# Statistics of the next image half a key block earlier, and sums of weight forms tied to running sums, in a fused GroupNorm and attention kernel

## The chip, the cores and the metric

The kernel runs on one core of one Trainium2 chip. The metric is the device time of one execution in microseconds (us); of several runs the median is taken. The engines are called PE (TensorE, the matmuls), PEld (its weight loads), DVE (VectorE), ACT (ScalarE), POOL (GpSimd) and SP (SyncE, which here only issues DMAs). Each of them runs its own instructions strictly in the order in which the compiled program has them, and waits on semaphores for the others.

## What is computed

One attention block over 16 images of 512 channels and 32 x 32 = 1024 positions, all in 32-bit floats:

```
x: (16, 512, 32, 32)
xn = GroupNorm(x, 8 groups) * gamma + beta
qkv = einsum('oc,bchw->bohw', qkv_w, xn) + qkv_b        # 1536 x 512 weights
q, k, v = 4 heads of 128 channels, 1024 positions each
attn = softmax(q k^T / sqrt(128))
out = proj_w (attn v) + proj_b                          # 512 x 512 weights
return x + out
```

## The kernel before

**The main loop.** The work on the scores sets the rhythm. A *step* is one block of 128 keys of one head of one image; 16 images x 4 heads x 8 blocks make 512 steps. A step has two halves of 512 queries each. In every half PE computes the scores `s` of this step (line 1669) and the weighted sum `po` of the step before (line 1766); ACT takes the exponential `p` of the scores (line 1675); DVE adds each full `p` to the running sum `tot` of the head (lines 1688 and 1690), from which the softmax denominators come. Between the scores and weighted sums of a half, PE gets its share of the other matrix products: the q, k and v products of the next image and the output projection (`pp`) of the previous image. These use fast matrix multiplication (Strassen's scheme on two levels for images 0 to 3, a scheme with three by three by two blocks, `thirds`, from image 4 on), so they need many sums: of input blocks (`home_A`, `home_B`, on DVE), of weights, and of products (`pp_r`, `qk_r`, `v_r`, on DVE), and copies out of PSUM on ACT (`pp_u`, `pp_z` and others, lines 655, 821 to 828).

**Which head does what.** For an image b of 1 to 14, head 0 finishes the q and k products of image b. Head 1 runs the 28 units of the projection of image b - 1, loads `x` of image b + 1, and takes that image's GroupNorm. Heads 2 and 3 run products for image b + 1.

**GroupNorm of the next image.** `stats_chunk` handles one of four chunks of 128 channels on ACT: a pass with an accumulated sum (line 329), two tiny scalings, and a pass with accumulated squares (line 335). Both passes write to a scrap tile `junk`. `stats_group` then has two parts on DVE. `gather` (lines 357 to 363) brings the results of all chunks together, combines them and ends with a power on POOL; it is bound behind the running sum of key block 3 of head 1. `scale` (lines 367 to 101) makes the factors `sc` and `sh`, bound behind the running sum of block 4. The eight normalisations (line 108, ACT) multiply and shift halves of each chunk, and use `sc` and `sh`.

**Weight forms.** Images 0 to 3 also build the weights for `thirds`, in spare tiles. `form_steps` makes sums of weight blocks, called forms: it loads blocks, adds six forms (line 1505), stores them (line 1512), adds five more in the same places, and stores these. There are four such chunks, in heads 3, 4, 6 and 7 (heads counted from the start; head 4 is head 0 of image 1). `inner_steps` takes eleven groups of forms: a load of a group (through `load_quads`, lines 1521 and 1533, SP), the making of four inner sums (lines 1541 to 1544, DVE) and a store (line 1562, POOL). The groups belong to heads 5, 8, 9, 10, 11, 12 and 13. `lay_builder` writes these steps into slots of half a key block, with the load four or five halves ahead of the sums.

**What sets the order.** The program text gives every instruction a place, but the order on each engine is made when the program is compiled: a planner goes through a model of the execution and lets each engine take, of what would be ready by its reckoning, what comes first by priority and place. So an instruction may be put ahead of its place in the text when the planner reckons that its inputs are there and the engine is free. `tc.issue_after(ins)` binds the instructions of a block that run on the engine of `ins` behind it in that engine's order; the helper `behind(one, unit)` does so for a unit, and `behind_exp` binds it behind the newest exponential. `tc.high_priority` moves an instruction forward among those that are ready. `added[b, h, j]` is the running sum of image b, head h, key block j (from block 2 on), and `max(added)` is the newest one that the text has reached.

**The plan of a head.** `plan_head` returns eight lists, one for each key block. The first half of a list runs after the first half of the step, the rest after the second. Empty entries (`None`) hold the lists at equal lengths. In head 1 the list of block 2 has four empty entries and that of block 3 three; the four statistics units go into these lists.

Of the kernel before, what the change touches and what calls it, by code (L numbers as in the profile page):

```python
# [231 lines left out]
def fast_path(ctx, tc, x, sources, out, consts, flag, dims):  # L232
# [1231 lines left out]
    def quads(n):  # L1464

        t = builder["tiles"]
        return t[n // 4][:, n % 4]
# [13 lines left out]
    def form_steps(p, c):  # L1481
        made = {}

        def load():
            for m, base in enumerate((0, 2 * C, C)):
                nc.sync.dma_start(
                    builder["tiles"][m // 2][:, ds(2 * (m % 2), 2)],
                    qkv_wT[:, ds(base + p * Q + c * P, P)].rearrange(
                        "(r k p) d -> p r k d", p=P, k=KC
                    ),  # L1490
                )

        def slot(f):
            k = order_a.index(f) % 6
            return quads(8 + k if k < 4 else 2 + k)

        def add(first, last):

            def of(what):
                return quads(2 * what[0] + what[1]) if isinstance(what, tuple) else made[what]  # L1500

            for f, op, a, e in FORMS_A[first:last]:
                eng = nc.vector
                made[f] = slot(f)
                (eng.tensor_add if op == "+" else eng.tensor_sub)(made[f], of(a), of(e))

        def send(first, last):
            for i in (first, first + 4):
                e = min(last, i + 4 if i == first else last)
                t = builder["tiles"][2 if i % 6 == 0 else 1]  # L1510
                t = t[:, : e - i] if i % 6 == 0 else t[:, ds(2, e - i)]
                nc.sync.dma_start(forms_kept[p, c][:, i:e], t)

        return (
            load, lambda: add(0, 6), lambda: send(0, 6), lambda: add(6, 11), lambda: send(6, 11)
        )

    def load_quads(p, g, c, w, eng):
# [50 lines left out]
    def lay_builder():  # L1569

        def at(head, half, step):
            s, h = divmod(half + 16 * head, 2)
            extras.setdefault((s, h), []).append(step)

        if old == B:
            return
        at(HEADS, 4, lambda: behind(added[max(added)], sum_biases))
        chunks = [(p, c) for p in range(PAIRS) for c in range(2)]
        for head, where, firsts, last in BUILD_A:
            if where:  # L1580
                at(head, firsts[0], lambda where=where: take(where))
            for first in firsts:
                for i, step in zip((0, 4, 7, 11, 14), form_steps(*chunks.pop(0))):
                    at(head, first + i, step)
            if last:
                at(head, 15, builder.clear)
        assert not chunks
        groups = [divmod(G, len(THIRDS)) for G in range(LATE)]
        turn = 0
        for run_ in BUILD_B:  # L1590
            first = True
            for head, where, firsts in run_:
                if where:
                    at(head, firsts[0] - 1, lambda where=where: take(where))
            slots = [
                16 * head + f for head, where, firsts in run_ for f in firsts
            ]
            mine, groups = groups[: len(slots)], groups[len(slots):]
            steps = []
            for k, (p, g) in enumerate(mine):  # L1600
                steps.append(inner_steps(p, g, k % 2))
            for k, t in enumerate(slots):
                load, make, send = steps[k]
                at(0, t, load)
                at(0, t + 5, make)
                at(0, t + 5, send)
            at(0, slots[-1] + 5, builder.clear)
        assert not groups
# [42 lines left out]
    inverse, rows_of, added, exps = {}, {}, {}, {}  # L1651
# [323 lines left out]
    def behind(one, unit):  # L1975
        with tc.issue_after(one.ins):
            unit()
# [4 lines left out]
    def plan_head(b, h):  # L1982

        plan = [[] for _ in range(NB)]
# [21 lines left out]
        elif h == 1:  # L2006
            if b > 0:
                spread(plan, [None] * 28, 0, NB)
                halfway.extend(paced(proj_groups(b - 1), 3))
                if flow:  # L2010
                    halfway[0] = flow.pop() + halfway[0]
            if b + 1 == B:
                plan[0].append(lambda: last_loads("x"))
            else:
                chunks = range(NCC) if b > 0 else range(KC, NCC)
                plan[0].append(lambda: load_x(b + 1, chunks))
                units = [
                    lambda c=c: behind_exp(lambda: stats_chunk(b + 1, c)) for c in chunks
                ]
                if b > 0:  # L2020
                    for i, u in enumerate(units):
                        plan[2 + i // 2].insert(0 if i % 2 == 0 else len(plan[2]), u)
                else:
                    spread(plan, units, 1, 3)
                gather, scale = stats_group(b + 1)
                if b == 0:
                    plan[3].append(gather)
                    plan[4].insert(0, scale)
                else:
                    plan[4].insert(0, gather)  # L2030
                    plan[5].insert(0, scale)
                for r in range(2):
                    units = [
                        lambda c=c, half=half: normalise(b + 1, c, half, b > 0 or c % 2 == 1)
                        for c in range(KC * r, KC * r + KC) for half in range(NH2)
                    ]
                    plan[5 + r] += units if b > 0 else [
                        lambda u=u: behind_exp(u) for u in units
                    ]
                if b + 1 < old:  # L2040
                    plan[6].append(lambda: x_sums(b + 1, (1,)))
            if b == 0:
                for part in range(2):
                    plan[1 + part].append(lambda part=part: behind(
                        latest["worst"], lambda: keep_kept("v", part, nc.sync)
                    ))
                plan[5].append(stage_proj)
        elif b + 1 == B:
            if h == 2:
                units = two_levels("last", "proj", b, lambda: late["two"], None)[0]  # L2050
                late["units"] = units[2:]
                products(plan, units[:2], NB, "last 2")
                plan[0].append(lambda: last_loads("w"))
                plan[0].append(ahead["last", "w"])
                plan[2].append(last_bias)
                plan[5].append(lambda: first_pair(b))
            else:
                os_[b, h] = opool.tile([P, N], F32, tag="o", name=f"o_{b}_{h}")
                products(plan, late["units"], NB, "last 3")
                plan[3].append(lambda: first_terms(b, 0))  # L2060
                plan[3].append(lambda: o_blocks(b))
                plan[4].append(lambda: first_terms(b, 1))
                plan[5].append(lambda: sums_of_b(ob[b], (2, 3), (0,)))
        elif b + 1 >= old:
            if h == 2:
                flow.extend(thirds(b + 1))
                spread(plan, [None] * 37, 0, NB)
                halfway.extend(flow[:16])
                del flow[:16]
        elif h == 2:  # L2070
            if b == 0:
                other_banks()
            spread(plan, [None] * 28, 0, NB)
            halfway.extend(paced(qk_groups(b + 1, 0), 4))

            plan[0].insert(2, lambda: x_sums(b + 1, (2,)))
            plan[1].append(lambda: x_sums(b + 1, (3,)))
            if b == 0:
                plan[3].append(lambda: behind(added[0, 2, 2], sum_proj))
                plan[4].append(  # L2080
                    lambda: behind(added[0, 2, 3], lambda: keep_kept("proj", 0, nc.gpsimd))
                )
        else:

            spread(plan, [None] * 28, 0, NB - 1)
            halfway.extend(paced(next_v.pop(), 3))

            plan[NB - 2].append(lambda: ahead[f"qk_{b + 1}_1"]())
            if b == 0:
                plan[1].append(lambda: keep_kept("proj", 1, nc.gpsimd))  # L2090
# [213 lines left out]
    plan = []  # L2304
    for s in range(steps + 1):
        units = []
        if s < steps:
            b, h, j = where(s)
            if j == 0:
                left = carry.pop() if carry else []  # L2310
                plan = plan_head(b, h)
# [9 lines left out]
        for half in range(NH2):  # L2321
# [21 lines left out]
            n = (len(units) + 1) // 2  # L2343
# [158 lines left out]
```

## Time and profile before

| | us |
|---|---|
| median of 3 runs (lowest, highest) | 3149.41 (3147.36, 3150.98) |
| the profiled execution | 3149.29 |
| its span, first to last instruction | 3147.7 |
| PE busy | 3115.7 |
| DVE busy | 2695.5 |
| ACT busy | 1724.7 |
| POOL busy | 471.1 |

The span lies 1.6 us under the time of the same execution. All lines of profile in this text come from that one execution; times in them count from its first instruction. A line of a timeline has the start, the length, the engine, the line of the kernel, the operation, the tiles (out<-in) with their shapes, the number of equal instructions merged into the row, and in brackets the idle time of the engine before it with what ended it. A row of the waits has who waited for whom, the total, the number of times and the longest. Matmuls of PE overlap each other, and so a row's length is longer than its share of the time: what counts is the distance between starts.

### The profile page before, as it was taken

The numbers are of one execution on the slowest core, as the hardware profiler recorded it, in microseconds if no ns is written. First come the engines' busy times: TensorE is split into PE (matmuls) and PEld (weight loads), VectorE is DVE, ScalarE is ACT, GpSimd is POOL, SyncE is SP. The second block draws the span as 40 slices with busy tenths as digits, with TensorE's granted clock in tenths as the row PEclk, the third lists the DMA queues.
The fourth block names the chain that finished last, engine by engine and source line by source line (L and its number), as shares of the span: only waits on it lengthen the run. The fifth ranks groups of instructions, "written<-read, shape, count | busy, mean of one in ns | idle before, by whom it ended". The sixth has DMA issues, their size and how long they took to land.

```text
span 3147.7 us, 38210 instructions
## 1 busy us (share of the span) xinstructions
PE 3115.7 (99%) x11934; PEld 2262.3 (72%) x11934; DVE 2695.5 (86%) x4604; ACT 1724.7 (55%) x3744; POOL 471.1 (15%) x792
## 2 busy tenths in 40 slices
PE   9999999999999999999999999999999999999999
PEld 7566676767777777777777777777777777777775
DVE  8987978789898897888978889788897888989887
ACT  3544546446565565656556565565555656556543
POOL 0121121121021110211102111121111111111110
PEclk9999999999999999999999999999999999999999
DMA  5566764665767656676666666676666666666761
GB/s 177 177 219 195 242 219 163 214 208 190 226 219 210 212 193 207 212 224 196 200 197 223 218 198 199 194 233 208 201 201 206 222 209 197 211 208 205 222 193 45
DMA packets 244062, 636.78 MB, mean 202 GB/s; under 512 B 32656, under 2 KB 77840, under 8 KB 243856
## 3 DMA queue, kind: packets, MB, share of 16 engines
q1 hardware_dynamic: 164912, 363.58, 37.3%
q0 software_dynamic: 66272, 236.38, 22.2%
q10 hardware_dynamic: 12672, 34.35, 3.7%
q8 instruction: 96, 1.57, 0.2%
q14 instruction: 110, 0.90, 0.1%
HBM read 462.49 MB, written 171.69 MB: 201 GB/s over the span
## 4 chain that ended last, share of the span: by engine, by line
PE 61%; ACT 5%; DVE 3%; issue 2%; DMA 0%; POOL 0%; ACTq 0%; POOLq 0%
PE s L1669 18%; PE po L1766 18%; PE t_x L1237 12%; PE t_y L1237 6%; PE t_z L1237 3%; PE pp_x L780 2%; ACT junk L329 1%; PE pp_y L780 1%; ACT junk L335 1%; DVE tot L1690 1%; ACT p L1675 1%; ACT x L108 1%; DVE pp_r L887 0%; PE pp_z L780 0%; DVE o L1779 0%
## 5 line engine op out<-in xcount | busy, mean ns | idle before, releaser
L1766 PE MATMUL po<-p,v 128*128 128x512 f32 x2048 | 1046.2, 592 | 0.0
L1669 PE MATMUL s<-qk,qk 128*128 128x512 f32 x2048 | 1046.0, 592 | 0.0
L1766 PEld LDWEIGHTS po<-p,v 128*128 128x128 f32 x2048 | 616.1, 301 | 376.2 <-issue 259.7
L1675 ACT ACTIVATE p<-s 128x512 f32<-128x512 f32 x1024 | 611.6, 597 | 498.7 <-PE s L1669 494.5
L1690 DVE TENSOR_TENSOR tot<-tot,p 128x1024 f32<-128x1024 f32 (+1 forms) x408 | 471.2, 1156 | 178.7 <-ACT p L1675 176.4
L1669 PEld LDWEIGHTS s<-qk,qk 128*128 128x128 f32 x2048 | 362.2, 189 | 59.1 <-issue 29.4
L1261 DVE TENSOR_TENSOR r<-t_y,t_u 128x342 f32<-128x342 f32 (+1 forms) x384 | 185.0, 482 | 138.1 <-PE t_y L1237 111.0
L1352 DVE TENSOR_TENSOR r<-r,r 128x684 f32<-128x684 f32 x264 | 225.7, 862 | 1.7
L1237 PE MATMUL t_x<-home_B,w 128*128 128x171 f32 x1008 | 187.7, 308 | 0.0
L1237 PE MATMUL t_x<-home_A,w 128*128 128x171 f32 x1008 | 187.7, 308 | 0.0
L1237 PEld LDWEIGHTS t_x<-home_A,w 128*128 128x128 f32 x1008 | 161.7, 189 | 30.2 <-issue 20.1
L1237 PEld LDWEIGHTS t_x<-home_B,w 128*128 128x128 f32 x1008 | 161.7, 189 | 30.2 <-issue 20.1
L780 PE MATMUL pp_x<-home_B,w_proj 128*128 128x256 f32 x630 | 168.3, 384 | 14.6 <-ACT pp_u L828 13.8
L1330 POOL DMA_DIRECT2D vd<-vu x48 | 34.8, 728 | 955.2 <-DVE vu L1322 955.2
L1061 POOL DMA_DIRECT2D v<-vd x240 | 140.7, 592 | 191.9 <-DMA x<-in_x 57.4
L780 PEld LDWEIGHTS pp_x<-home_B,w_proj 128*128 128x128 f32 x630 | 117.4, 190 | 59.2 <-ACT pp_u L828 23.7
L1124 DVE TENSOR_TENSOR f<-x 128x684 f32<-128x684 f32 x168 | 143.9, 856 | 0.8
L1197 ACT COPY t_u<-t_x 128x342 f32<-128x342 f32 x192 | 78.7, 410 | 118.9 <-PE t_x L1237 112.6
L1237 PEld LDWEIGHTS t_z<-f,w 128*128 128x128 f32 x528 | 89.5, 190 | 51.8 <-issue 34.4
L108 ACT ACTIVATE x<-x,sh,sc 128x512 f32<-128x512 f32 x120 | 92.6, 809 | 27.7 <-DVE sh L101 26.0
L1322 DVE STREAM_TRANSPOSE vu<-vt 128x256 f32<-128x256 f32 x192 | 104.2, 643 | 0.0
L1203 ACT ACTIVATE t_u<-t_x,bias 128x171 f32<-128x171 f32 x192 | 72.3, 404 | 57.1 <-PE t_x L1237 57.0
(383 smaller groups left out, 5107.4 us busy)
## 6 DMA issues: line engine op xcount, KB each, us to landing
w<-kept SPq DMA_DIRECT2D x182, 512.0 KB, 3.9
w<-kept SPq DMA_DIRECT2D x182, 384.0 KB, 4.1
kept_t<-home_A POOLq DMA_DIRECT2D x96, 342.0 KB, 3.9
home_B<-kept_t SPq DMA_DIRECT2D x96, 342.0 KB, 3.0
rinv<-row ACTq DMA_DIRECT2D x63, 512.0 KB, 5.7
x<-in_x POOLq DMA_DIRECT2D x60, 512.0 KB, 8.3
v<-vd POOLq DMA_DIRECT2D x240, 128.0 KB, 7.3
out_y<-y_c POOLq DMA_DIRECT2D x60, 512.0 KB, 3.9
```

The source lines that it names most:

```text
L108: return self.nc.scalar.activation(xn, x, AF.Identity, bias=sh[:, i], scale=sc[:, i])
L780: latest["product"] = nc.tensor.matmul(acc[:, ts(i, Q)], have["w"][t][:, i, slot, :], inner(i, bn), start=(first and i == 0), stop=True, s ...
L1061: nc.gpsimd.dma_start(vs[b, pair][ts(q, BLK), half].rearrange("m h (k i) j -> m (h k) (i j)", k=n), rows.rearrange("(k m) (q e) -> q m k e ...
L1124: (eng.tensor_add if op == "+" else eng.tensor_sub)(made[f], of(a), of(c))
L1237: latest["product"] = nc.tensor.matmul(acc[:, ts(i, H3)], wts[G, t][:, i, slot, :], moving, start=(start and i == 0), stop=True, skip_grou ...
L1261: nc.vector.tensor_add(dst, view(a), view(c))
L1322: nc.vector.transpose(u[:, h].rearrange("p (q i j) -> p j q i", q=n, i=BLK)[:, ds(2 * q, 2)], made["vt"][:, h, ts(part, Q)].rearrange("p ( ...
L1352: (nc.vector.tensor_add if add else nc.vector.tensor_sub)(at(o), a, c)
L1669: latest["score"] = nc.tensor.matmul(sc, ks[b, h][:, ts(j, P)], qs[b, h][:, ts(half, HALF)], start=True, stop=True)
L1675: exps[s] = nc.scalar.activation(ps[s][:, ts(half, HALF)], sc, AF.Exp, scale=SCALE)
L1690: added[b, h, j] = nc.vector.tensor_add(tot[b, h][:, i], tot[b, h][:, i], ps[s][:, i])
L1766: summed = nc.tensor.matmul(po[half], v_block(b, h, j), ps[s][:, i], start=(j == 0), stop=(j == NB - 1),)
```

## The change

Three places.

In `form_steps`, the first six sums of a chunk of forms are bound behind the newest running sum of exponentials. In `lay_builder`, the four inner sums of each group are bound in the same way. Before, only the order of the data and the planner's reckoning placed them. Loads and stores, and the last five sums of a chunk, have no new tie of their own. In slots of the first half of a step the newest running sum in the text is that of the step before; in the second half it is the step's own, with one exception: in block 6 of head 1 of images 1 to 14 the running sum stands behind these steps in the text, so that the newest is that of block 5.

In `plan_head`, the four statistics units of the next image, for images 1 to 14, move from blocks 2 and 3 (first and second half each) to the second half of block 1, both halves of block 2 and the first half of block 3. The bounds of `gather` and `scale` stay as they are.

```diff
@@ form_steps
         return (
-            load, lambda: add(0, 6), lambda: send(0, 6), lambda: add(6, 11), lambda: send(6, 11)
+            load, lambda: behind(added[max(added)], lambda: add(0, 6)),
+            lambda: send(0, 6), lambda: add(6, 11), lambda: send(6, 11),
         )
@@ lay_builder
                 load, make, send = steps[k]
                 at(0, t, load)
-                at(0, t + 5, make)
+                at(0, t + 5, lambda make=make: behind(added[max(added)], make))
                 at(0, t + 5, send)
@@ plan_head, head 1
                 if b > 0:
                     for i, u in enumerate(units):
-                        plan[2 + i // 2].insert(0 if i % 2 == 0 else len(plan[2]), u)
+                        n = plan[(3 + i) // 2]
+                        n.insert(0 if i % 2 else len(n), u)
```

## The prediction

> **What bounds the kernel now.** I read the page's busy shares first, then the waits of TensorE (PE), then the places of those waits in the timelines of PE, ScalarE (ACT) and VectorE (DVE).
>
> ```profile
> PE 3115.7 (99%) x11934; PEld 2262.3 (72%) x11934; DVE 2695.5 (86%) x4604; ACT 1724.7 (55%) x3744; POOL 471.1 (15%) x792
> PE pp_x L780 <- ACT pp_u L828: 13.8, 14, 1.0
> PE qk_y L780 <- DVE qk_r L813: 8.7, 5, 4.9
> PE v_y L780 <- DVE v_r L813: 2.5, 3, 0.8
> DVE groups L357 <- ACT junk L335: 14.0, 14, 1.0
> DVE a_v L1541 <- DMA a_o<-kepta: 9.8, 3, 6.2
> ```
>
> (The rows under the first are those of the waits: who waits for whom, us in total, times, the longest.) PE is the bound: it is busy in 3115.7 us, and nearly all its waits are of three kinds. The largest comes exactly 14 times, once in each of the images 1 to 14, whose head 1 holds the statistics of the next image. The second comes 5 times, while the weight forms are built (images 1 to 3). One place of the first kind, image 7, on PE:
>
> ```profile
> 1496.86 1.02 PE L1766 MATMUL po<-p,v 128*128 128x512 f32 x2
> 1497.94 1.13 PE L780 MATMUL pp_x<-home_B,w_proj 128*128 128x256 f32 x4
> 1498.90 0.59 PE L780 MATMUL pp_x<-o,w_proj 128*128 128x256 f32 x2
> ...
> 1504.93 0.59 PE L780 MATMUL pp_x<-home_B,w_proj 128*128 128x256 f32 x2
> 1505.36 1.02 PE L1669 MATMUL s<-qk,qk 128*128 128x512 f32 x2
> 1506.22 1.02 PE L1766 MATMUL po<-p,v 128*128 128x512 f32 x2
> 1508.22 0.70 PE L780 MATMUL pp_x<-home_B,w_proj 128*128 128x256 f32 x2 [0.98 <-ACT pp_u L828]
> 1509.45 1.02 PE L1669 MATMUL s<-qk,qk 128*128 128x512 f32 x2
> ...
> 1519.19 0.75 PE L1237 MATMUL t_x<-home_A,w 128*128 128x171 f32 x4
> ```
>
> Matmuls overlap, so a stall is priced by starts, not by the gap. Undisturbed, a pair of 512 columns takes 0.86 us (1505.36 to 1506.22) and a pair of 256 takes 0.43 (1504.93 to 1505.36). After 1506.22, `pp_x` was due at 1507.08 and, with one more pair of 256 between (`pp_y`), the next `s` at 1507.94. It came at 1509.45: 1.51 us are lost, not 0.98. A second loss hides under the threshold of the waits: after `po` at 1496.86 the group at 1498.90 was due at 1498.58, so 0.32 us. Together 1.83 us an image.
>
> Why it waits, on ACT and DVE:
>
> ```profile
> 1474.67 0.60 ACT L1675 ACTIVATE p<-s 128x512 f32<-128x512 f32 x1 [0.27 <-PE s L1669]
> 1476.40 0.59 ACT L821 COPY pp_r<-pp_x 128x512 f32<-128x512 f32 x1 [1.12 <-PE pp_x L780]
> 1478.98 0.60 ACT L1675 ACTIVATE p<-s 128x512 f32<-128x512 f32 x1 [1.10 <-PE s L1669]
> ...
> 1491.62 1.15 ACT L335 ACTIVATE junk<-x,sums 128x1024 f32<-128x1024 f32 x1
> ...
> 1494.49 1.08 ACT L329 ACTIVATE junk<-x 128x1024 f32<-128x1024 f32 x1
> ...
> 1497.17 0.46 ACT L828 ACTIVATE pp_u<-pp_x,projb_sb 128x256 f32<-128x256 f32 x1
> ...
> 1506.29 1.52 ACT L108 ACTIVATE x<-x,sh,sc 128x512 f32<-128x512 f32 x2 [1.85 <-DVE sh L101]
> 1507.72 0.45 ACT L828 ACTIVATE pp_u<-pp_x,projb_sb 128x256 f32<-128x256 f32 x1
> ```
>
> ```profile
> 1492.49 1.22 DVE L1690 TENSOR_TENSOR tot<-tot,p 128x1024 f32<-128x1024 f32 x1
> ...
> 1497.34 0.11 DVE L357 MEMSET groups<- 128x64 f32 x1 [1.02 <-ACT junk L335]
> ...
> 1499.15 1.22 DVE L1690 TENSOR_TENSOR tot<-tot,p 128x1024 f32<-128x1024 f32 x1
> ...
> 1503.21 0.24 DVE L367 STREAM_TRANSPOSE groups<-groups 128x64 f32<-128x64 f32 x1 [0.18 <-POOL groups L363]
> ...
> 1506.10 0.15 DVE L101 TENSOR_TENSOR sh<-beta_sb,t 128x4 f32<-128x4 f32 x1
> ...
> 1517.12 0.51 DVE L1155 TENSOR_TENSOR home_A<-x,home_A 128x342 f32<-128x342 f32 x1
> ```
>
> The first statistics chunk starts right behind the exponential of key block 2, half 0, at 1478.98. The fourth runs from 1494.49 to 1497.17 and holds the `pp_u` eviction behind it: that is the 0.32. The gather on DVE idles 1.02 us for that chunk and starts at 1497.34. Its chain ends with `sh` at 1506.10. Two normalisations (L108) stand ahead of `pp_u` on ACT and wait for `sh`, and so `pp_u` starts at 1507.72 and PE at 1508.22.
>
> **The statistics, half a key block sooner.** No instruction is added or removed in images 1 to 14; four chunks move from the slots (2,0), (2,1), (3,0), (3,1) (key block, half) to (1,1), (2,0), (2,1), (3,0). I expect chunks two to four to take today's places of one to three, since each is bound behind the exponential of its slot. The last then ends where the third ends today, at 1491.62 + 1.15 = 1492.8, 4.4 us sooner. The gather stays behind the running sum of key block 3 and `scale` behind that of block 4. The first of these sums ends at about 1493.6 (1492.49 + 1.13 to the next start), the second at about 1500.3. So the gather can start 3.7 us sooner. The transposition at 1503.21 can start up to 2.9 us sooner, and `sh` at about 1503.2. Two normalisations of 0.72 each then start no later than 1504.5, behind the exponential of block 5, and `pp_u` starts at about 1505.9. PE needs it 0.50 us ahead of its own start, at 1506.58 for the due time 1507.08. The spare is 0.7 us, and both losses go: 14 x 1.83 = 25.6 us.
>
> What the moved first chunk costs: it comes behind the exponential at 1474.67, where ACT idles 1.12 and 1.10 us up to the next exponential, 2.2 in all, and a chunk takes 2.7 (1494.49 to 1497.17). Between evictions it can hold one up. The ends are 0 and one whole square, 1.15 us, an image (0 to 16 us); the nearest row is today's chunk that holds up `pp_u` for 0.32, so I take 14 x 0.32 = 4.5. Below zero it can't go: PE loses nothing at that place now. The chunk needs its `x`:
>
> ```profile
> 1463.21 2.18 POOL L293 DMA_DIRECT2D x<-in_x  x4
> x<-in_x POOLq DMA_DIRECT2D x60, 512.0 KB, 8.3
> ```
>
> Issued at 1463.21, landed some 8.3 us later, 1471.5; wanted at about 1475.2. Were this cover gone, ACT would stand with the exponentials and evictions behind it, and PE with it.
>
> **The sums of weight forms, tied.** Four first sums of forms (six instructions each) and eleven makes (four each), all on DVE, in images 0 to 3. Today each runs where the planner thought its load had landed. One place, from the timelines of PE and DVE and, in the last row, the busy times of a stretch (PE, its weight loads, DVE, ACT, POOL, then the granted clock):
>
> ```profile
> 267.43 0.70 PE L780 MATMUL qk_x<-x,w 128*128 128x256 f32 x2
> 273.05 2.08 PE L780 MATMUL qk_y<-xt,w 128*128 128x256 f32 x4 [4.93 <-DVE qk_r L813]
> ...
> 278.27 0.59 PE L780 MATMUL qk_z<-x,w 128*128 128x256 f32 x2
> 265.56 0.43 DVE L1541 TENSOR_TENSOR a_v<-a_o 128x256 f32<-128x256 f32 x1 [6.21 <-DMA a_o<-kepta]
> 265.90 0.75 DVE L981 SCALAR_TENSOR_TENSOR qk<-qk_r,qkb_sb,qk_r 128x512 f32<-128x512 f32 x1
> 273.00:278.30 5.30, 5.25 (x9) 2.88 (x10) 5.30 (x8) 0.60 (x1) 1.08 (x2) 0.51 0.62 200
> ```
>
> DVE stood 6.21 us for a load, the evictions `qk_r` queued behind it, and PE stood 4.93 us. By starts, `qk_z` was due at 267.43 + 0.43 + 3 x 0.86 = 270.44 (one pair of 256, a group of four, `s` and `po`) and came at 278.27: 7.83 us, since PE then ran at a granted clock of 0.51. Of the 8.7 us in the waits' row 3.8 are left for the other four, taken as they are. The ties move the sums behind the running sums of their own slots, a good part of a head later for this make, long after the loads, so that all five waits should go: 7.8 + 3.8 = 11.6 us.
>
> What the ties add: a tied sum queues behind a running sum, which waits for the exponential, and it loses the idle time ahead of that sum. Six of the eleven makes fall into head 1 of images 1 to 3, behind the sums of blocks 2 and 5. There DVE is full, as the same view shows for the end of head 1 of image 7 (the stretch's length, then PE, weight loads, DVE: 12.50 of 12.50):
>
> ```profile
> 1503.84:1516.34 12.50, 11.52 (x31) 6.66 (x31) 12.50 (x17) 9.59 (x16) 2.21 (x3) 1.00 0.52 171
> ```
>
> Behind the tied sums wait the next running sums, the gather, and the first `home_A` sums of head 2, for which PE waits. Four instructions at 0.34 (265.56 to 265.90) are 1.36 us; six times that is 8.2. The ends are 0 and 8.2; I take half, 4.1. Their DMAs move too: the results go by POOL, ahead of `out_y` and the gather's power, and the next group's load goes by SP behind that store. A make behind block 2 comes before the sum of block 3 (1492.49 in image 7), ten microseconds ahead of the power, which ends just before 1503.21; one behind block 5 comes after it. So I cost the DMAs at nothing; if a make came late, the power and `sh` would wait for its store on POOL.
>
> **The sum.** The profiled execution took 3149.29 us, 0.1 below the median of the three runs, so both are the same ruler. 3149.3 - 25.6 - 11.6 + 4.5 + 4.1 = 3120.7 us. With both added costs at zero it is 3112.1; if the waits on `v_r` (2.5) shift away too, 3109.6.
>
> **Rivals.** *DVE sets the pace.* In this case PE gets ahead and then waits for DVE, which gains only its 1.02 us of idle time an image. For it speaks that DVE works without a gap up to the first sums of head 2. Against it: the second `home_A` sum is done at 1517.63 and PE uses it at 1519.19. That spare of 1.56 plus the 1.02 covers the 1.83. The price: 3149.3 - 14.0 - 11.6 + 4.1 = 3127.8. [...]
>
> *The normalisations wait again.* Planned ahead of an eviction by the planner's earlier `sh`, they meet a chip on which it isn't there, and a 1.51 returns: 3149.3 - 4.5 - 11.6 + 4.5 + 4.1 = 3141.8.
>
> *The tied sums pay back what they save* (a new wait on a load or a held `home_A`): 3132.3, with 11.6 struck from the sum.
>
> *Slower.* The planner puts four normalisations instead of two ahead of `pp_u`, and `sh` comes no sooner than today, since `scale` is still bound to block 4 and DVE carries the makes. Then `pp_u` starts 1.43 us later than today (two more at 0.72), 14 x 1.43 = 20.0: 3149.3 + 20.0 - 4.5 - 11.6 + 4.5 + 4.1 = 3161.8. It decides against the change from an `sh` that leaves PE 0.54 us an image worse than today ((4.5 + 11.6 - 8.6) / 14). With four ahead today's PE time needs `sh` at 1506.10 - 1.43, so the point lies at about 1505.2.
>
> *No effect*: the planner's order comes out the same where it matters: 3149.3.
>
> **How the numbers follow.** The forecast 0.47, DVE's pace 0.12, waiting again 0.10, paid back 0.08: faster 0.77. No effect 0.07. Slower 0.16. A difference under 0.2%, 6.3 us, can't be told from none. The range starts at 3109 and reaches to 3150; outside lies the slower case.
>
> **What would show it.** Right: the wait of `pp_x` on `pp_u L828` is gone, the gather starts within 1 us of the end of block 3's running sum, L108 begins within 11 us of the end of that sum (1493.6 and 1504.5 above), `qk_y` waits on `qk_r` are gone and no clock below 1 stands between 265 and 280. Wrong: a new 14-fold wait of PE anywhere in head 1, or `home_A` waits at the start of head 2; waits of L1541 on DMA with PE waits behind them.

## The result and the profile after

The changed kernel takes 3124.21 us (median, 3123.72 to 3126.18); the kernel before took 3150.12 us beside it. The ratio is 0.992, 95% interval 0.9903 to 0.9938. The profiled execution took 3124.18 us, with a span of 3122.6 us against 3147.7 before: 25.1 us less. The forecast was 3120.7 us, so 3.5 us less than came.

First the busy shares of the changed kernel from the page, then the waits of TensorE (PE): who waits for whom, us in total, times, the longest.

```profile
PE 3106.7 (99%) x11934; PEld 2262.9 (72%) x11934; DVE 2693.1 (86%) x4604; ACT 1720.8 (55%) x3744; POOL 471.6 (15%) x792
PE pp_x L780 <- ACT pp_u L828: 6.6, 14, 0.5
PE v_y L780 <- DVE v_r L813: 2.6, 3, 0.9
PE t_y L1237 <- DVE r L1261: 1.1, 2, 0.6
```

The five waits of `qk_y` on `qk_r` (8.7 us) are gone from this list. The 14 waits of `pp_x` on `pp_u` are not: they are half as long. Image 7 again, from the timelines of PE and ACT (start, duration, idle time ahead and what ended it):

```profile
1480.86 1.03 PE L780 MATMUL pp_x<-home_B,w_proj 128*128 128x256 f32 x4
1481.72 0.59 PE L780 MATMUL pp_x<-o,w_proj 128*128 128x256 f32 x2
...
1489.04 1.02 PE L1767 MATMUL po<-p,v 128*128 128x512 f32 x2
1490.45 0.70 PE L780 MATMUL pp_x<-home_B,w_proj 128*128 128x256 f32 x2 [0.39 <-ACT pp_u L828]
1490.98 0.64 PE L780 MATMUL pp_y<-o,w_proj 128*128 128x256 f32 x2
1491.46 1.02 PE L1670 MATMUL s<-qk,qk 128*128 128x512 f32 x2
```

```profile
1485.90 0.82 ACT L108 ACTIVATE x<-x,sh,sc 128x512 f32<-128x512 f32 x1 [1.23 <-DVE sh L101]
...
1487.34 0.81 ACT L108 ACTIVATE x<-x,sh,sc 128x512 f32<-128x512 f32 x1
...
1488.52 1.51 ACT L108 ACTIVATE x<-x,sh,sc 128x512 f32<-128x512 f32 x2
1489.93 0.47 ACT L828 ACTIVATE pp_u<-pp_x,projb_sb 128x256 f32<-128x256 f32 x1
```

At block 4 the 0.32 us are gone (0.86 from 1480.86 to 1481.72); in two of the 14 images, 2 and 6, 0.2 to 0.3 of them stay. At block 6 `pp_x` was due at 1489.04 + 0.86 = 1489.90 and `s`, two pairs of 256 later, at 1490.76; it came at 1491.46. So 0.70 us stay, where 1.51 + 0.32 were. Summed by such starts over the 14 images, 11.9 us stay of 25.6. Ahead of `pp_u` now stand four normalisations (L108), not two.

The same stretch on DVE:

```profile
1475.63 1.22 DVE L1691 TENSOR_TENSOR tot<-tot,p 128x1024 f32<-128x1024 f32 x1
1476.81 0.11 DVE L357 MEMSET groups<- 128x64 f32 x1
...
1481.64 1.22 DVE L1691 TENSOR_TENSOR tot<-tot,p 128x1024 f32<-128x1024 f32 x1
...
1485.71 0.15 DVE L101 TENSOR_TENSOR sh<-beta_sb,t 128x4 f32<-128x4 f32 x1
...
1487.04 2.36 DVE L1644 TENSOR_TENSOR y_c<-pp_r,y_c 128x1024 f32<-128x1024 f32 x2
1489.32 1.22 DVE L1645 TENSOR_TENSOR y_c<-y_c,pp_r 128x1024 f32<-128x1024 f32 x1
1490.45 0.42 DVE L813 TENSOR_TENSOR pp_r<-pp_y,pp_u 128x256 f32<-128x256 f32 x1
```

The gather (L357) follows the running sum of block 3 at once; its 1.02 us of idle time are gone. `sh` comes 4.07 us after the start of block 4's sum (1481.64), where it came 6.95 after (1499.15 to 1506.10): the 2.9 us sooner that were forecast. The last row is the one to remember: `pp_r`, the second eviction of the same product group, starts on DVE at 1490.45, behind three residual additions (`y_c`). It, too, is late: `pp_y`, which waits for it, was due at 1490.33 and comes at 1490.98.

The builder, by the busy times of a stretch (length, PE, weight loads, DVE, ACT, POOL, granted clock):

```profile
265.00:280.00 15.00, 15.00 (x47) 10.12 (x46) 15.00 (x23) 6.97 (x13) 1.07 (x2) 1.00 0.76 263
```

PE no longer stands there, and the clock stays at 1.00. By starts, the `qk_y` waits of the images 1 to 3 ("the builder" below) cost 0.4 us where they cost 13.2.

### The profile page after: what moved, and what is told of

Same layout as the page of the kernel before. It is cut to its first block, busy times and chain, and to the rows that moved or that the text cites. A ratio compares the mean times of both kernels' runs of the same rounds, so it can differ in the third digit from the quotient of the medians.

```text
span 3122.6 us, 38158 instructions
## 1 busy us (share of the span) xinstructions
PE 3106.7 (99%) x11934; PEld 2262.9 (72%) x11934; DVE 2693.1 (86%) x4604; ACT 1720.8 (55%) x3744; POOL 471.6 (15%) x792
## 5 line engine op out<-in xcount | busy, mean ns | idle before, releaser
L108 ACT ACTIVATE x<-x,sh,sc 128x512 f32<-128x512 f32 x120 | 94.5, 814 | 20.5 <-DVE sh L101 18.8
```

The costliest lines, as they stand in the source:

```text
L108: return self.nc.scalar.activation(xn, x, AF.Identity, bias=sh[:, i], scale=sc[:, i])
```

## The experiments

**The two halves alone: stats_only and ties_only.** The kernel before with the one or the other part of the change.

```
stats_only:
-  plan[2 + i // 2].insert(0 if i % 2 == 0 else len(plan[2]), u)
+  n = plan[(3 + i) // 2]
+  n.insert(0 if i % 2 else len(n), u)
ties_only:
-  load, lambda: add(0, 6), ...
+  load, lambda: behind(added[max(added)], lambda: add(0, 6)), ...
-  at(0, t + 5, make)
+  at(0, t + 5, lambda make=make: behind(added[max(added)], make))
```

> The kernel before with one part of the change: the four statistics chunks begin half a key block sooner; the first sums and makes of weight forms stay untied. Theory A (the parts add up, and the profile after shows what the statistics part leaves): of the 25.6 us an equal 13.8 us go and 11.9 stay, because normalisations still stand ahead of the last projection eviction of head 1; the builder's stalls of 13 us stay as before: about 3149.3 - 13.8 = 3135.5 us, pp_x waits on pp_u L828 14 times for about 0.5 us each. Theory B (the forecast's step was right by itself, and only the makes that sit on VectorE spoil it): the images 4 to 14, which hold no make, show no loss in head 1 here either way, so they would fall to 0 and the time to about 3124. Theory C (the ties did it all): 3149.

> The kernel before with the other part of the change: first sums and makes of weight forms tied behind the running sums, the statistics where they were. Theory A (the parts add up): the five qk_y waits on qk_r go, 12.8 us, and the 14 waits of pp_x on pp_u stay with 1.83 us each: about 3149.3 - 12.8 = 3136.5 us. Theory B (the six makes in the full head 1 of images 1 to 3 cost 1.36 us each where the statistics end late): up to 8.2 us come back, all in images 1 to 3, about 3140 to 3144.5; the loss in these images would be 3.2 or more instead of 1.83.

Measured: stats_only 3135.85 us against 3148.09 beside it (ratio 0.996, 0.9947 to 0.9974), ties_only 3138.2 us (0.9967, 0.9955 to 0.9978). The spans fell by 13.4 and 11.1 us, 24.5 together, against 25.1 for the whole change: the parts add up. Waits of PE in stats_only, then in ties_only:

```profile
PE qk_y L780 <- DVE qk_r L813: 7.3, 6, 4.6
PE pp_x L780 <- ACT pp_u L828: 6.8, 14, 0.5
```

```profile
PE pp_x L780 <- ACT pp_u L828: 13.8, 14, 1.0
PE t_y L1237 <- DVE r L1261: 1.3, 3, 0.5
```

Theory A holds in both, and B falls in both. Without any tied make, stats_only loses 0.7 to 1.2 us in every image, so the makes did not spoil the forecast's step. In ties_only the images 1 to 3 lose 1.5 and 0.3 us, just as the others: six makes in a full head 1 cost nothing while the statistics are late. By starts, ties_only loses 1.2 us more than the kernel before at two places where `t_y` waits, in images 3 and 4. The one in image 4 is no price of the ties: stats_only, which has none, loses 0.8 us more there.

**Both evictions: norms_behind.** The normalisations that stood ahead of `pp_u` are taken from there.

```
-  nc.scalar.copy(dst[:, i, :], src[:, i, :])
+  latest["evicted"] = nc.scalar.copy(dst[:, i, :], src[:, i, :])
...
-  nc.scalar.activation(
+  latest["evicted"] = nc.scalar.activation(
...
-  plan[5 + r] += units if b > 0 else [
-      lambda u=u: behind_exp(u) for u in units
-  ]
+  plan[5 + r] += [
+      lambda u=u: behind(latest["evicted"], u) for u in units
+  ] if b > 0 else [lambda u=u: behind_exp(u) for u in units]
```

> The changed kernel with one more tie: the first two groups of normalisations of the next image (planned for block 5 and after) are bound behind the newest projection eviction of ScalarE, so that none stands between the exponential of block 5 and the last projection eviction of head 1. Theory A (the normalisations ahead of that eviction are what is left of the loss): pp_u starts at once when its matmul is done, the 14 waits go and with them the 11.9 us that are left: about 3124.2 - 11.9 = 3112 us. Theory B (VectorE sets the pace): the gain appears as new waits of TensorE at the start of head 2, on home_A, or of L108 later than its readers; 3118 to 3124. Theory C (slower): the normalisations, pushed behind that eviction, make the next image's projections wait: 14 x up to 1.4 = 20, 3144 at most, with waits of t_x on home_A.

Measured: 3124.34 us, no gain over the changed kernel. Its waits of PE, and the place in image 7 on PE and DVE:

```profile
PE pp_y L780 <- DVE pp_r L813: 8.2, 14, 0.7
```

```profile
1489.91 0.59 PE L780 MATMUL pp_x<-home_B,w_proj 128*128 128x256 f32 x2
1490.93 0.70 PE L780 MATMUL pp_y<-o,w_proj 128*128 128x256 f32 x2 [0.43 <-DVE pp_r L813]
1491.46 1.02 PE L1670 MATMUL s<-qk,qk 128*128 128x512 f32 x2
...
1475.64 1.22 DVE L1691 TENSOR_TENSOR tot<-tot,p 128x1024 f32<-128x1024 f32 x1
...
1490.46 0.42 DVE L813 TENSOR_TENSOR pp_r<-pp_y,pp_u 128x256 f32<-128x256 f32 x1
```

`pp_x` now comes on time (1489.91), the 14 waits on `pp_u` are gone, and `s` still comes at 1491.46. The next matmul, `pp_y`, waits for DVE's `pp_r` and starts 0.47 us after it. Theory A falls, and B holds, at another place than it named: head 1 itself. In the changed kernel two evictions were late by nearly the same: one held `pp_x` to 0.55 us behind its due time of 1489.90, the other holds `pp_y` here to 0.59 behind 1490.34. The view of waits named the one that PE met first.

**Was that so before the change? before_norms.** The same tie in the kernel before, without either part of the change.

> The kernel before, neither part of the change in it, with the normalisations bound behind the newest projection eviction as in norms_behind. Theory A (already in the kernel before two evictions were late together: pp_u on ScalarE, and pp_r on VectorE, which started at 1508.44 in image 7 and released pp_y 0.47 us later, at 1508.91 against a due time of 1507.51): the 14 waits of pp_x on pp_u L828 go and 14 waits of pp_y on pp_r L813 of about 1.1 us take their place; no gain, 3146 to 3150 us. Theory B (the forecast's reading: ScalarE's eviction alone made the 1.51 us): 14 x 1.51 = 21 us are saved, 3128 us.

Measured: 3147.41 us against 3148.27 beside it (ratio 0.9999, 0.999 to 1.0008). Its waits, and the place in image 7 on PE and DVE:

```profile
PE pp_y L780 <- DVE pp_r L813: 17.5, 14, 1.3
```

```profile
1505.17 0.59 PE L780 MATMUL pp_x<-home_B,w_proj 128*128 128x256 f32 x2
...
1490.59 1.22 DVE L1690 TENSOR_TENSOR tot<-tot,p 128x1024 f32<-128x1024 f32 x1
...
1506.54 0.42 DVE L813 TENSOR_TENSOR pp_r<-pp_y,pp_u 128x256 f32<-128x256 f32 x1
...
1507.02 0.70 PE L780 MATMUL pp_y<-o,w_proj 128*128 128x256 f32 x2 [1.25 <-DVE pp_r L813]
```

Theory A: clearing the wait on which the forecast rested was worth nothing by itself. By starts the loss is 1.51 us an image as ever. The trace before had it, in a row of DVE that the prediction leaves out:

```profile
1508.44 0.41 DVE L813 TENSOR_TENSOR pp_r<-pp_y,pp_u 128x256 f32<-128x256 f32 x1
```

1508.44 + 0.47 is 1508.91, for a `pp_y` due at 1507.51.

DVE's own queue sets how late it is. In image 7, from the start of block 3's running sum to this eviction, DVE takes 15.95 us in the kernel before (1492.49 to 1508.44) and the same in before_norms (1490.59 to 1506.54), where ScalarE's order is another. With the statistics sooner it takes 14.82 us, again with and without the tie on ScalarE (1475.63 to 1490.45 in the changed kernel, 1475.64 to 1490.46 in norms_behind).

**Other ways to a sooner `sh`: scale_3 and stats_more.** scale_3 binds `scale` behind block 3's running sum; stats_more begins the chunks another half key block sooner. Both start from the changed kernel.

```
scale_3:     lambda: part(4 if b > 1 else 3, scale)  ->  lambda: part(3, scale)
stats_more:  n = plan[(3 + i) // 2]; n.insert(0 if i % 2 else len(n), u)
         ->  n = plan[(2 + i) // 2]; n.insert(len(n) if i % 2 else 0, u)
```

> The changed kernel with the second half of the gather chain (scale) bound behind the running sum of key block 3, as the gather is, and no longer behind that of block 4. Theory A (the lateness of sh is what is left): sh comes one running sum, 1.22 us, or more sooner, the 1.23 us that ScalarE waits for it in image 7 go, and with them the 11.9 us: about 3112 us. Theory B (the planner moves the normalisations as far ahead as sh, and their place on ScalarE is what costs): they now stand ahead of the projection evictions of block 4 too and hold those up; the loss of 0.85 us an image stays or grows to the 1.5 of the kernel before: 3124 to 3133 us.

> The changed kernel with the four statistics chunks another half key block sooner, in (1,0), (1,1), (2,0), (2,1). Theory A (after the change the gather is held by the running sum of block 3 and no longer by the chunks): sh and the loss stay as they are, 3124 us, give or take what two more chunks ahead of evictions cost (up to 14 x 0.3 = 4 us). Theory B (the chunks still hold the gather): sh comes sooner and part of the 11.9 us goes, 3113 to 3120 us.

Measured: scale_3 3144.86 us, stats_more 3125.01 us. Waits of PE in scale_3, and block 4 of image 7 on PE, ACT and DVE:

```profile
PE pp_y L780 <- DVE pp_r L813: 9.8, 14, 1.0
PE pp_x L780 <- ACT pp_u L828: 7.6, 14, 0.5
```

```profile
1491.63 0.70 PE L780 MATMUL pp_y<-home_A,w_proj 128*128 128x256 f32 x2 [0.56 <-DVE pp_r L813]
...
1491.68 1.52 ACT L108 ACTIVATE x<-x,sh,sc 128x512 f32<-128x512 f32 x2 [2.12 <-DVE sh L101]
...
1490.34 0.25 DVE L367 STREAM_TRANSPOSE groups<-groups 128x64 f32<-128x64 f32 x1 [0.46 <-POOL groups L363]
...
1490.89 0.68 DVE L813 TENSOR_TENSOR pp_r<-pp_y,pp_u 128x512 f32<-128x512 f32 x1
```

For scale_3, B had the direction, but its worst case (3133) was too good: by starts 0.8 to 1.2 us an image are lost at block 4 and 1.2 to 1.4 from the end of block 5 to block 6. Its mechanism came: a sooner `sh` in the plan drew two normalisations ahead of block 4's evictions on ACT, where they waited 2.12 us for it. That is the forecast's rival "the normalisations wait again" in kind, from another edit. But it isn't what PE lost at block 4, where the wait is over (1491.63) before they start (1491.68): PE waits there for DVE's `pp_r`, ahead of which `scale` now stands, and `scale` itself waits 0.46 us for POOL's power. stats_more is theory A: the gather was no longer held by the chunks.

**The price of one stall: one_make.** The kernel before with only the make tied that had stood 6.21 us for its load.

```
-  at(0, t + 5, make)
+  at(0, t + 5, (lambda make=make: behind(added[max(added)], make)) if t == 80 else make)
```

> The kernel before with one single make tied behind the running sum, the first group's, which stood 6.21 us for its load; all else is as before. Theory A (that place costs TensorE 7.9 us by starts, the gap and the lower clock after it): about 3148.1 - 7.9 = 3140.2 us. Theory B (only the gap of 4.93 us counts, the lower clock is made good elsewhere): 3143.2 us. Theory C (the make moves its wait to the next group): 3147 or more, with a new wait of qk_y on qk_r.

Measured: 3141.3 us against 3149.81 (ratio 0.9974, 0.9963 to 0.9985); the span fell by 7.9 us. The stretch of the stall:

```profile
265.00:280.00 15.00, 15.00 (x47) 10.04 (x47) 14.60 (x25) 7.42 (x14) 1.07 (x2) 1.00 0.63 212
```

Theory A by the span and by the starts; the ratio's interval (4.7 to 11.7 us) can't tell 7.9 from 4.9. By starts this place gives back 7.7 us; elsewhere the waits in image 3 shrank by 1.4 us and others grew by 1.1, so that the span shows nearly this place alone. The gap of 4.93 us and the slow matmuls behind it are one price.

**Order or amount of work on DVE: norms_and_adds, adds_behind, home_too.** If DVE's `pp_r` is late, is DVE too full, or is it in a bad order? norms_and_adds is norms_behind with two residual additions (one of which had stood ahead) and the running sum of block 5 bound behind `pp_r`; adds_behind has that order on DVE alone; home_too also lets the first `home_A` sums of head 2 go ahead of the sum of block 7.

```
norms_and_adds, adds_behind:
   done("c21", ...):
+    pending.extend([lambda: None] * 6)
   finish(which, a, c):
-    nc.vector.tensor_add(t, a, t)
-    nc.vector.tensor_add(t, t, c)
+    with tc.issue_after(latest["outer" if which == "c21" else "finish"].ins) \
+            if which in ("c21", "c12") else nullcontext():
+        nc.vector.tensor_add(t, a, t)
+    latest["finish"] = nc.vector.tensor_add(t, t, c)
   running_sum of block 5, head 1: emitted with block 6's, behind latest["finish"]
home_too, besides (two places):
-  tc.issue_after(added[b - 1, 1, NB - 1].ins)
+  tc.issue_after(added[b - 1, 1, NB - 2].ins)
```

> norms_behind, and on VectorE the two residual additions of the third quarter (y_c, 1.14 us each) and the running sum of block 5 are bound behind the eviction pp_r of the last product group, ahead of which they stood in norms_behind. Theory A (of two evictions that TensorE needs at the end of head 1, one on ScalarE and one on VectorE, both were late by the same 0.7 us, so that clearing one showed only the other): with both clear pp_r starts 1.1 us sooner, at 0.5 us ahead of the due time of pp_y, both 14-fold waits go and with them about 11 us: 3113 us. Theory B (VectorE as a whole sets the pace: it is full from the gather to head 2, and reordering it only moves the wait): the loss comes back as waits of TensorE on other evictions of VectorE or on home_A, 3120 to 3126 us.

> The changed kernel with the order of VectorE of norms_and_adds, but with the normalisations where the changed kernel has them, ahead of the last projection eviction of ScalarE. Theory A (two evictions, equally late): ScalarE's is still 0.7 us late, so the wait of pp_x on pp_u L828 stays 14 times and nothing is gained: 3124 us, up to 3128 as the planner now puts one of head 2's sums f (0.8 us) ahead of pp_r. Theory B (VectorE's eviction alone was what counted): about 3113 us.

> norms_and_adds, and the first home_A sums of head 2 are bound behind the running sum of block 6 in place of that of block 7, so that one sum f (0.78 us) and one home_B sum (0.43 us) no longer stand ahead of the second of them. Theory A (VectorE has the time, only its order is late): the second home_A sum is done 1.2 us sooner, 0.5 us ahead of its due time, and the 0.74 to 0.93 us an image go: about 3124.2 - 11 = 3113 us, with no 14-fold wait of TensorE left. Theory B (VectorE's sum of work in the stretch from the gather to head 2 is the bound): the same 0.7 to 0.9 us come back at a later place of head 2, on f, home_B or r, and the time stays at 3120 to 3125 us.

Measured: norms_and_adds 3124.22 us, adds_behind 3132.5 us, home_too 3115.05 us. First norms_and_adds, its waits and image 7:

```profile
PE t_x L1239 <- DVE home_A L1157: 7.0, 12, 0.9
PE qk_x L780 <- DVE home_A L745: 1.1, 2, 0.6
```

```profile
1488.83 0.42 DVE L813 TENSOR_TENSOR pp_r<-pp_y,pp_u 128x256 f32<-128x256 f32 x1
...
1499.97 0.51 DVE L1157 TENSOR_TENSOR home_A<-x,home_A 128x342 f32<-128x342 f32 x1
...
1500.54 0.85 PE L1239 MATMUL t_x<-home_A,w 128*128 128x171 f32 x4 [0.48 <-DVE home_A L1157]
```

Head 1 has no loss left there, and the same 0.74 us stand at the start of head 2, on `home_A`: theory B at that step. adds_behind says less: its 14 waits on `pp_u` stayed as expected (7.0 us), but one of head 2's sums `f` came ahead of `pp_r` and stood 0.55 us for a normalisation, which made a second loss that I had priced too low (3128). Then home_too, its page and waits, and image 7:

```profile
PE 3103.1 (100%) x11934; PEld 2265.1 (73%) x11934; DVE 2694.5 (87%) x4604; ACT 1722.7 (55%) x3744; POOL 471.6 (15%) x792
PE v_y L780 <- DVE v_r L813: 2.6, 3, 0.9
PE t_y L1239 <- DVE r L1263: 1.9, 4, 0.7
```

```profile
1496.17 0.51 DVE L1157 TENSOR_TENSOR home_A<-x,home_A 128x342 f32<-128x342 f32 x1
...
1497.29 0.74 PE L1239 MATMUL t_x<-home_A,w 128*128 128x171 f32 x4
```

No 14-fold wait is left, and 9.2 us of span are gained over the changed kernel (3122.6 to 3113.4); the ratio to the kernel before is 0.9891 (0.9875 to 0.9908). Theory A: DVE does the same work in it (2694.5 us against 2693.1) and had the time. It was the order in three places, and two of the three gained nothing (3124.34, 3124.22) until the last was done; the last alone was not run. This version beats both kernels.

**Do the orders need the sooner statistics? before_orders.** All three orders in the kernel before.

> The kernel before, neither part of the change in it, with all three orders of home_too (normalisations behind the eviction, two residual additions and the sum of block 5 behind pp_r, home_A behind the sum of block 6). Theory A (the late statistics still cost VectorE 1.2 us of idle time an image at the gather and 0.32 at block 4, so part of the loss stays whatever the order, and the builder's 13 us stay): of 25.6 us 8 to 17 stay, 3132 to 3141 us; then the earlier statistics of the change are needed for the rest. Theory B (the three orders do all that the earlier statistics do): the head's 25.6 us go but for the 4.5 at block 4, about 3128 us.

Measured: 3145.2 us against 3148.27 (ratio 0.9988, 0.9979 to 0.9997). Its waits, and the gather on DVE in image 7:

```profile
PE pp_y L780 <- DVE pp_r L813: 10.0, 14, 0.7
DVE groups L357 <- ACT junk L335: 13.7, 14, 1.0
```

Theory A in direction, but the time lies above its range (3132 to 3141). The gather's idle time stays, DVE is late by it, and 0.31 us at block 4 and 0.98 at block 6 are still lost in each image. I had expected 8 to 17 us to stay; by starts it is 18 (14 x 1.29), and in most images some 0.2 us more is lost in head 3, before a `t_y`. So the three orders alone gain 3 us by the medians (6.0 by the spans of two single executions), the change alone 25, and the orders on top of the change 9 more. The gain of the orders depends on the sooner statistics, as it would if the idle time of DVE had to go first.

## Why the prediction was right, and where it was not

The time came within 0.2% of the forecast, but that is luck: the terms were wrong in size and offset each other. By the time alone, the rival "DVE sets the pace" (3127.8) was 3.6 us above the measured time, as near as the forecast, 3.5 below it; only the mechanism tells the two apart. Of the five signs that were to show the forecast right, four came. The first, on which its largest term rested, did not: the wait of `pp_x` on `pp_u` is still there.

- **The statistics (25.6 forecast): 13.7 measured.** All the steps up to `sh` came as written: the chunks took the places of their predecessors, the gather starts right behind block 3's sum, `sh` comes 2.9 us sooner. The step that failed is "two normalisations then start no later than 1504.5, `pp_u` starts at about 1505.9, the spare is 0.7 us, and both losses go". Four normalisations came ahead of `pp_u`. And even without them (norms_behind) nothing is gained, since the step looked at one of the two evictions that the product group needs. DVE's `pp_r` held `pp_y` 1.4 us behind its due time already before (before_norms).
- **The rival "DVE sets the pace" was right for this part.** It said that only DVE's idle time of 1.02 us an image is gained, 14.0 us in all; 13.7 came. DVE's stretch from block 3's sum to `pp_r` fell by 1.13 us, and did not depend on ScalarE's order. It had the place wrong: PE waits in head 1; only when head 1 was clear (norms_and_adds) did `home_A` hold it. The waits show that DVE ended last there once the normalisations were out of the way (`pp_y` on `pp_r`: 8.2 us in norms_behind, 17.5 in before_norms). The high occupancy of DVE did not mean that no time was left on it: home_too gains 9.2 us with the same 86 to 87%.
- **The rival "the normalisations wait again"** happened (four of them stand ahead of `pp_u`, which is 0.5 us late) and was not what decided.
- **The builder (11.6 forecast): 12.8.** The large place was right to 0.1 us (7.83 forecast; 7.7 by starts and 7.9 by the span in one_make). The four small waits cost 5 us by starts and not the 3.8 of the waits' row.
- **A `t_y` wait that was not in the sum: 0.9 back.** Most of it is in image 4. There four inner sums of image 4's own products stand 1.61 us for their load on DVE, and `r`, for which `t_y` waits, queues behind them. The change does not tie these sums, and stats_only, without any tie, has the same wait (1.68 us). Why DVE stands longer there than in the kernel before (0.86 us) is not shown.
- **The rival "the tied sums pay back what they save"** did not come: none of the tied makes waits for its load any more (12.9 us in four waits before).
- **The moved first chunk (4.5 forecast): nothing.** No loss stands at blocks 1 and 2 in the trace after. The lower end was right.
- **The makes in head 1 (4.1 forecast): 0.9 at most.** The images 1 to 3 lose 3.14 us together in head 1 of the changed kernel and 2.25 in stats_only. Images that hold no make differ by up to 0.3 us each between these two runs, so even this may not come from the makes.
- **The rivals "slower" and "no effect"** did not come. Four normalisations did stand ahead of `pp_u`, as "slower" has it, but `sh` came 2.9 us sooner.

The sum with the measured terms is 3149.3 - 13.7 - 12.8 + 0.9 = 3123.7 us, against 3124.18 (what the makes cost is inside the 11.9 that stay). The forecast took 11.9 us too much for the statistics, and 0.3 too little for the builder and the `t_y` wait together; it also charged 8.6 for additions of which the 11.9 already hold all that was found. That makes 3.0 us; 3.5 show.

## What to carry to other kernels

A wait names the release that came last, not the one that came next to last (13.8 us on `pp_u` in the kernel before; 17.5 us on `pp_r` in before_norms, where those were gone): before a wait is priced as gone, work out from the timelines when every other input of the waiting engine's next instructions is ready, and take the smaller gain. An engine that is busy with hardly a gap need not be the bound (in image 7 of the changed kernel DVE was busy in 13.89 of the 14.06 us from 1476.81 to 1490.87, and home_too, with the same work on it, is 9.2 us of span shorter); first look whether something that nobody needs yet stands in its queue ahead of what the bound engine waits for. When several queues are late by about the same time, clearing one can show no gain at all (norms_behind 3124.34 us, against 3124.21 for the changed kernel), and only a run with all of them cleared tells whether there was any to be had (home_too 3115.05).

## What the runs showed of the hardware

One stall of PE cost far more than its gap. In image 1, 4.93 us of waiting cost 7.8 us by starts, and one_make, which clears it, is 7.9 us of span shorter: the granted clock was 0.51 for the 5.30 us behind the gap. It was 1.00 in the gap's stretch from 270 to 271 us and 0.50 in that from 271.40 to 273. Where that wait is gone (one_make, ties_only, the changed kernel) the clock is 1.00 over the stretch from 265 to 280; stats_only, with a wait of 4.6 us there, has 0.77, as the kernel before has. In before_orders, whose longest wait of `qk_y` is 4.0 us, the mean clock of the profiled run is 0.999, as in the kernel before, against 1.000 in those three. The shorter waits of the kernel before left the clock at 1.00: one of 1.58 us (1.00 from 245.68 to 251.00), one of 1.74 us (1.00 from 673.43 to 679.00) and the 14 of 0.98 to 0.99 us (1.00 from 1508.22 to 1513.22 in image 7, and so in each). That trace has no wait of PE between 1.74 and 4.93 us.
